# Merge, second norm and output rows of a two-layer graph attention kernel turned on VectorE and by DMA instead of on TensorE

## The chip, the cores and the metric

The kernel runs on 1 core of one Trainium2 chip. The metric is the device time of one launch in microseconds (us), read as the median of the runs. A core has TensorE (PE, with its weight loads PEld), VectorE (DVE), ScalarE (ACT), GpSimd (POOL), and SyncE (SP), which here only issues DMAs. All values are fp32.

## The reference, cut to what matters

16 graphs of 1024 nodes with 256 features share one adjacency matrix. Each goes through two residual blocks:

```python
h = maximum(layernorm(x), 0)                  # first norm
r = relu(h @ mlp1_w + mlp1_b)                 # 256 -> 512
a = elu(attention(r, no mask, W_fc))          # dense attention, 512 wide
r = elu(a) + r                                # the merge
r = relu(r @ mlp2_w + mlp2_b)                 # 512 -> 256, the output rows
a = elu(attention(r, adj, W_hand))            # masked attention A
x = x + relu(elu(a) + r)
h = maximum(layernorm(x), 0)                  # second norm
x = x + relu(attention(h, adj, L1_W))         # masked attention B
```

An attention is softmax over sources j of leaky_relu(f1[i] + f2[j]), times the projected rows.

## The kernel before

A graph's rows lie in SBUF either as nodes on the 128 partitions (natural) or as features on the partitions (turned). Matmuls that project features need the turned form, so the kernel turns data several times per graph. With 1024 nodes there are NT = 8 tiles of P = 128 nodes, in NH = 2 halves of TH = 4 tiles; 256 features are FC = 2 chunks, 512 are HC = 4.

**Stages of one graph.** `BlockNorm` or `Norm` makes the first norm; `Dense.mlp1` (line 743) makes `resT`, turned. `Dense.project` (754) makes natural rows `h_nat`. The dense attention has no mask, so it is not done as products of 1024 x 1024 weights (but for half of graph 0): the sources are ranked by their score (`rank`, 802), scattered in sorted order to HBM (`scatter`), read back, turned into running sums (`sum_before`, `sum_behind`), and written as tables; each node then fetches two rows by indirect DMAs on GpSimd (`gather`, 925; lines 934 in the profile). `mean` (951) combines them to natural rows `hp` of 513 values. `merge` (1001) turns four tiles of `hp` by four PE transposes into a PSUM bank per feature chunk, takes min with 0 on DVE (1008), two exponentials on ACT (1009, 1010), which give elu(elu(.)) up to a constant; `merge_end` (1013) joins them on DVE (1016) and adds them to `resT` on POOL (1017). `mlp2` (1019) makes `oT`, turned. `Masked.project` (605) uses `oT` as the stationary operand. `natural` (1030) turns `oT` back by four PE transposes per pair of tiles and ACT copies it out as `o_nat` (1040). The masked attention A makes weights on DVE (`weight`, 663, eight buffers deep) and products on PE (`product`, 672); `combine` and `add` (705, 706) add `o_nat` on POOL, `update` adds to x. The second norm is a `Norm`: statistics, `center` (526) on DVE, `turn` (529) with PE transposes (536) into PSUM, relu copy on ACT (540). Masked attention B follows the same way with `wl_sb`.

**First norm of graphs 3 to 15.** This one is a `BlockNorm` already: ACT centers and applies relu (565), DVE's transpose turns each 32 x 32 block in place (572), and 16 DMAs per half, issued by SP (582), carry each block to its place, in runs of 128 bytes.

**What sets the order.** The work of all graphs is a list of steps with due times in us, written with `at(name, lo, hi, steps)`; a table `SHIFT` corrects single due times. PERIOD (142) is the nominal distance of two graphs. The list is sorted by due time and traced in that order. PE, DVE, ACT and SP each keep exactly that order (`manual_schedule`, line 1397), and POOL is held to it as well (scatters among themselves excepted). So a due time decides only what stands ahead of what in an engine's queue. An instruction that is not ready holds back all that is behind it on its engine. The stages of several graphs are interleaved: while one graph is in its masked attentions, the next is in its table stage, and the one after that in its first projection.

**Buffers that matter.** `tr` PSUM has 2 banks, `mm` PSUM 4. `hT` has one buffer, shared in time by `oT` and the turned second norm. `onat` has one, `hp` four tiles, `hn` four tiles.

Of the kernel before, what the change touches and what calls it, by code (L numbers as in the profile page):

```python
# [28 lines left out]
D_MIN = 1.0e-7  # L29
SHIFT = {  # L30
    "end dense_begin1": (-2.54,),
    "end dense_begin2": (-0.99,),
    "end dense_begin4": (9.79, 10.84, 0, 0, 0, -3.05, 0, -5.96,),
    "end dense_begin5": (-23.89, -15.67,),
    "end dense_begin6": (-20.81, 0, -12.64, -10.02, -11.47, -12.26,),
    "end dense_begin7": (-3.07,),
    "end dense_end1": (-7.17, -1.95,),
    "end dense_end2": (-6.38, -6.38, -6.38, -6.38,),
    "end dense_rows1": (-10.51, -6.24, -6.82, 0, 0, 0, 0, -4.24,),
    "end dense_sums1": (-48.96,),  # L40
    "end dense_sums10": (-21.95,),
    "end dense_sums2": (8.53, 0, 0, 3.76, -8.53, -12.13, -7.88, -5.24,),
    "end dense_sums3": (-9.59, -12.4,),
    "end dense_sums4": (-7.91, -7.91, -7.91, -7.91, -3.45, -3.45, -3.45, -3.45,),
    "end dense_sums6": (10.61,),
    "end dense_sums7": (-3.22, -4.43, -3.58, -3.26, 0, -0.77, 0, 4.02,),
    "end dense_sums8": (3.76,),
    "end dense_sums9": (2.37,),
    "end early_gathers2": (10.03, 10.03,),
    "end early_gathers3": (-5.29, 18.84, 14.56, 18.48,),  # L50
    "end early_gathers4": (0, 0.45, 0, 0, 10.2, 15.36, 8.86, 10.63,),
    "end first_mlp1": (-7.09, 0, 0, -10.32,),
    "end first_mlp2": (-4.41, -4.41, -4.41, -4.41,),
    "end masked_first1": (-9.1,),
    "end masked_first10": (0, 0.7, -4.33, -3.67, -2.03, -1.81, -3.41,),
    "end masked_first11": (0, 0, -4.93, -4.17, -2.96, -1.43, -4.36, -0.47,),
    "end masked_first12": (0, -1.5,),
    "end masked_first13": (0, 0, -4.74, -4.15, 0, 0.69, 1.51, 0.6,),
    "end masked_first14": (0.61, 3.4, -2.77, -2.71, 0.32, 3.65, 1.3, 0.83,),
    "end masked_first15": (-2.98,),  # L60
    "end masked_first16": (0.15,),
    "end masked_first2": (-8.7,),
    "end masked_first4": (-7.99,),
    "end masked_first5": (-9.93, -3.59, -1.25,),
    "end masked_first7": (-18.06, 0, 3.52, 24.98,),
    "end masked_first9": (-2.7, -2.7, -2.7, -2.7, -2.7, -2.7, -2.7, -2.7, -1.13, -0.9, -1.12,
        -1.51, -1.92, -2.78, -3.21, -3.56, -4.22, -2.23, -1.85, -1.53, -1.76, -2.17, -2.28, -2.05,
        -5.73, -5.67, -4.93, -4.1, -4.46, -4.69, -5.08, -4.71, -7.38, -5.64, -6.02, -5.94, -4.67,
        -3.38, -2.99,),
    "end masked_second1": (0, 0, 0, 0, 0, 0, -2.7, -2.7, -2.7, -2.7, -2.7, -2.7, -4.75, -4.45, 0,  # L70
        0, 0, 0, 0, 1.61, 1.54, 3.47, 3.07, 3.3, -3.32, -2.79, 0, 0, 0, 0.67, -6.09, -6.45, -6.84,
        -3.49, 0, 2.45,),
    "end masked_second2": (0, 0, 0, 0, 0, 0, 3.2, 2.96, 0.23, 0.23, 0, 2.22,),
    "end masked_second3": (-0.67, -0.43, 0, 0, -0.54, 3.58, 2.58, 1.28,),
    "end masked_second4": (0, 0, 0, 0, 0, 2.18, 2.56, 4.8,),
    "end masked_second5": (14.49, 8.09, 12.75, 21.36, 24.19, 12.45,),
    "end masked_second6": (0, 17.47,),
    "end merges1": (-2.65, -5.36, -2.83, -5.06, 0, 2.68, 2.67, 0.66,),
    "end merges2": (-2.65, -5.24, 5.1, 1.49, 3.05, 1.93, 4.16, 11.78,),
    "end scatters1": (8.25, 10.06, -7.13, -3.44, -5.23, -10.63, 0, -8.12,),  # L80
    "end second_mlp1": (1.82, 4.66, 8.88, 11.17,),
    "end second_mlp2": (-9.26, -9.26, -9.26, -9.26, -9.26, -9.26, -9.26, -9.26,),
    "end second_mlp3": (-9.24,),
    "end second_norm1": (-4.45, -1.81, -4.63, -4.57, -4.39, -5.31, -5.93, -6.31,),
    "end second_norm2": (-6.82,),
    "end second_norm3": (-6.84,),
    "end second_norm4": (-7.95,),
    "end second_norm5": (-8.56, -3.63, -2.16, -3.25, -3.33, -6.23, -7.8,),
    "end second_norm6": (-7.46,),
    "end second_norm8": (0, 0, 0, 0, 31.85,),  # L90
    "end turn_at1": (-3.4, 0, 0, -4.89, -0.78, -0.78, -0.78, -0.78,),
    "end turn_at2": (0, 0, 0, 0.78, -1.37, -1.37, -1.37, -1.37,),
    "end weights a": (-5.34, -5.34, -5.34, -5.34, -5.34, -5.34, -5.34, -5.34, -1.3, -1.76, -8.73,
        -6.94, -1.68, -8.23, 0, 1, 0.15, 0, 0, 0, -7.3, 1.55, 0, 0, -2.46, -12.74, -3.66, -1.38,
        -1.88, -1.72, -2.61, -5.89, -4.74, -29.97, -2.33, -12.21, -4.28, -4.33, -3.77, -7.66,),
    "end weights b": (-7.6, -7.02, -8.62, -8.6, -3.43, -3.15, -2.16, 1.28, -7.9, -5.17, -3.12,
        1.84, 1.74, 2.72, -12.96, -7.11, -4.91, -8.89, -1.88, -2.69, -5.62, -3.89, -12.92, 1.63,
        -4.21, 0, -3.79, 0, 0, 2.74, 0.99, 2.24, -1.57, 0, -4.21, -0.92, -1.67, 0, 3.31, 2.71,
        -4.74, -4.74, -4.74, -4.74, -4.74, -4.74, -4.74, -4.74,),
    "first dense_begin1": (-4.48,),  # L100
    "first dense_begin2": (-2.87,),
    "first dense_begin3": (-3.83,),
    "first dense_begin4": (0, 0, 0, 0, 3.89, 0, 0, -2.44,),
    "first dense_begin5": (-21.03,),
    "first dense_begin6": (0, -31.1, -17.42, 4.95, -36.3, -14.56,),
    "first dense_begin7": (82.37,),
    "first dense_begin8": (7.54,),
    "first dense_end2": (0, 0, 2.75, 0, 0, 0, 0.57,),
    "first dense_rows1": (-3.65, 7.43, 4.91, 2.63, 0, -6.58, -11.11, -13.44,),
    "first first_mlp1": (-2.95, 0, 23.52,),  # L110
    "first first_mlp2": (1.92, 1.92, 1.92, 1.92,),
    "first first_norm3": (-20.91, -5.96, -6.07, -3.96, -21.09, -13.48, -23.18, -24.87,),
    "first first_norm4": (-5.5,),
    "first first_norm5": (0, -5.77, -1.25, -11.69,),
    "first first_norm6": (0, 0, 0, 0, 11.68, 18.8, 11.89,),
    "first first_norm7": (24.88, 40.1, 28.15, 35.87,),
    "first first_norm8": (26.12, 24.89, 20.85, 23.62,),
    "first gathers1": (0, 0, 0, 0, -16.12, 15.29, 10.43, 15.06,),
    "first gathers2": (5.92, 5.92, 5.92, 5.92, -11,),
    "first masked_first1": (-5.71,),  # L120
    "first masked_first10": (0, 0, 0, -2.4, -2.31, -5.55, -2.46, -3.12,),
    "first masked_first11": (0, 0, 0.71, -2.32, -2.78, -4.87, -2.51, -3.56,),
    "first masked_first13": (1.26, -0.54, -1.35, -6.25, -3.52, -7.85, -6.5, -7.52,),
    "first masked_first14": (3.16, 4.53, -1.81, -2.01, -1.61, -2.14, -7.33, -7.83,),
    "first masked_first15": (-5.06,),
    "first masked_first16": (-8.17,),
    "first masked_first4": (-5.61,),
    "first masked_first9": (0, 0, 0, 0, 0, 0, 0, 0, -1.71, -1.71, -1.71, -1.71, -1.71, -1.71,
        -1.71, -1.71, -2.98, -2.63, -1.7, -2.54, -2.61, -2.64, -3.51, -4.14, -3.57, -3.57, -3.57,
        -3.57, -3.57, -3.57, -3.57, -3.57,),  # L130
    "first masked_second1": (-14.06, -8.94, -9.49, -4.7, -3.33, -3.94, -2.72, -2.72, -2.72, -2.72,
        -2.72, -2.72, 0, 0, 0, 0, 0, 0, -2.18, -2.01, -2.79, -3.55, -3.29, -2.87,),
    "first masked_second2": (-3.14, -3.14,),
    "first masked_second3": (-3.5, -2.57, 0, 0.84, 7.19, 0.39, 33.41, 2.67,),
    "first masked_second4": (0, 0, 20.11, 7.6, 22.77, 6.57, 53.75, 28.92,),
    "first masked_second6": (32.22, 65.4,),
    "first merges1": (6.27, -3.15, 0, 3.13, 0, -2.78,),
    "first merges2": (3.91, -4.92, 0, 1.15, 3.24, -0.48, -0.83, 2.62,),
    "first scatters1": (0, 0, 0, 0, 0, 4.56, 0, -6.46,),
    "first second_mlp1": (-1.44, 0, 17.3, 6.53,),  # L140
    "first second_mlp2": (-5.85, -5.85, -5.85, -5.85, -5.85, -5.85, -5.85, -5.85,),
    "first second_norm1": (0, 2.5, 3.9, 8.4, 1.01, 0, 0.77,),
    "first second_norm2": (4.83,),
    "first second_norm6": (2.78,),
    "first second_norm7": (-8.87,),
    "first second_norm9": (-2.96,),
    "first start51": (-9.84,),
    "first turn_at1": (-11.5, -11.5, -11.5, -11.5, -7.26, -7.26, -7.26, -7.26,),
# [130 lines left out]
def fast_path(ctx: ExitStack, tc: tile.TileContext, alarm, x, adj, w1, b1, w2, b2, w_fc, a_fc,  # L279
# [942 lines left out]
    def last(b, n=1):  # L1222
        return b >= NB - n
# [633 lines left out]
```

## Time and profile before

| what | value |
|---|---|
| median of 2 runs | 2250.68 us (2250.66 to 2250.7) |
| the profiled execution, its own time | 2251.37 us |
| its span, first to last instruction | 2249.6 us |
| mean granted TensorE clock | 0.998 |
| distance of two graphs (issues of `rowsb` by SP at 514.41 and, ten graphs on, at 1858.81) | 134.4 us |
| HBM read and written | 226.88 MB and 126.29 MB |

How to read it: a line of the groups names line, engine and operation, out<-in, shape and count, then the group's busy time in us and the mean of one instruction in ns, then the idle time ahead of it and what ended it. The mean of a matmul is its latency; matmuls overlap, so the slot that one takes is read from the distance of two starts in the timeline. A line of the windows gives the busy us of each engine in that stretch. The chain of waits is followed back from the last instruction to whatever released each step.

### The profile page before, as it was taken

To read this page: it belongs to the slowest core of one execution; us is meant where nothing else is said; L and a number is where in the kernel's file an instruction comes from. 1 tells how busy PE (TensorE), PEld (TensorE's weight loads), DVE (VectorE), ACT (ScalarE), POOL (GpSimd) and SP (SyncE) were. 2 spreads that over 40 slices of the span, in tenths; PEclk is the share of its full clock that TensorE was granted. 3 is DMA by queue.
4 is the path that set the end of the run, shared out by engine and by line. 5 is a ranking of instruction groups with operands and counts; after the bars stand their busy time and mean duration, and the time that the engine had idled before them with its cause. 6 is when DMAs were issued, how large, how long until landed. Compare 5 with 4: busy or idle time off the path is not lost.

```text
span 2249.6 us, 31025 instructions
## 1 busy us (share of the span) xinstructions
PE 2207.2 (98%) x9754; PEld 1723.4 (77%) x9754; DVE 1643.1 (73%) x4535; ACT 1259.6 (56%) x2797; POOL 954.4 (42%) x1212
## 2 busy tenths in 40 slices
PE   7999999999999999999999999999999999999997
PEld 5767777787877878787787877878787787877776
DVE  7677676777867678776776867677786776858765
ACT  5355745547365564756557375564746557365542
POOL 1163425263452536425263452636435263543620
PEclk9999999999999999999999999999999999999999
DMA  5568466675766757566685666757566585645700
GB/s 197 159 175 196 114 208 154 186 183 148 197 123 200 187 168 190 137 196 148 192 191 147 189 127 194 188 177 189 130 205 144 185 197 153 164 125 169 178 22 28
DMA packets 263870, 368.95 MB, mean 164 GB/s; under 512 B 124352, under 2 KB 175880, under 8 KB 259600
## 3 DMA queue, kind: packets, MB, share of 16 engines
q1 hardware_dynamic: 217088, 202.72, 31.9%
q0 software_dynamic: 45952, 163.99, 28.9%
q8 instruction: 80, 1.31, 0.3%
q14 instruction: 94, 0.77, 0.1%
q10 hardware_dynamic: 656, 0.17, 0.0%
HBM read 226.88 MB, written 126.29 MB: 157 GB/s over the span
## 4 chain that ended last, share of the span: by engine, by line
PE 75%; DVE 6%; DMA 2%; POOL 2%; ACT 1%; issue 1%; POOLq 0%; DVEq 0%; ACTq 0%; SPq 0%
PE oa L677 17%; PE h L762 16%; PE ob L677 14%; PE m L1024 8%; PE m L748 6%; PE pa L614 4%; PE pb L614 3%; PE hpT L1006 2%; DMA got<-coarse,k 2%; DVE attb L667 1%; PE carry L918 1%; PE on L1038 1%; PE nt L536 1%; DVE stats L516 1%; DVE hp L959 1%
## 5 line engine op out<-in xcount | busy, mean ns | idle before, releaser
L677 PE MATMUL ob<-hmb,attb 128*128 128x257 f32 x2048 | 463.9, 380 | 2.2 <-DVE attb L667 1.9
L762 PE MATMUL h<-wfc_sb,resT 128*128 128x257 f32 x2048 | 462.8, 379 | 0.0
L677 PE MATMUL oa<-hma,atta 128*128 128x258 f32 x2048 | 459.9, 382 | 1.8 <-DVE atta L667 1.5
L677 PEld LDWEIGHTS ob<-hmb,attb 128*128 128x128 f32 x2048 | 383.9, 190 | 67.2 <-issue 12.3
L677 PEld LDWEIGHTS oa<-hma,atta 128*128 128x128 f32 x2048 | 384.8, 190 | 59.3 <-DVE atta L667 2.9
L762 PEld LDWEIGHTS h<-wfc_sb,resT 128*128 128x128 f32 x2048 | 380.1, 189 | 59.1 <-issue 7.4
L705 POOL TENSOR_TENSOR posa<-posa,onat 128x256 f32<-128x256 f32 x118 | 106.7, 904 | 546.1 <-ACT posa L693 487.6
L667 DVE SCALAR_TENSOR_TENSOR attb<-rowsb,qwdb,edge 128x256 f32<-128x256 f32 (+1 forms) x536 | 292.1, 563 | 34.6 <-PE ob L677 28.6
L667 DVE SCALAR_TENSOR_TENSOR atta<-rowsa,qwda,edge 128x256 f32<-128x256 f32 (+1 forms) x520 | 257.3, 524 | 51.4 <-DMA rowsa<-row_a 35.6
L934 POOL DMA_INDIRECT got<-coarse,k x124 | 203.4, 1640 | 90.9 <-DMA got<-fine,k 56.6
L748 PE MATMUL m<-hT,w_sb 128*128 128x512 f32 x512 | 236.6, 596 | 1.9 <-ACT rb L719 1.1
L1024 PE MATMUL m<-resT,w_sb 128*128 128x512 f32 x512 | 228.3, 593 | 1.0 <-POOL resT L1017 1.0
L719 ACT ACTIVATE rb<-ob,recb 128x256 f32<-128x256 f32 x128 | 58.5, 474 | 274.9 <-DVE recb L717 248.9
L1017 POOL TENSOR_TENSOR resT<-resT,e 128x512 f32<-128x512 f32 x128 | 165.5, 1295 | 104.9 <-DVE e L1016 96.7
L692 ACT ACTIVATE ea<-oa,reca 128x256 f32<-128x256 f32 x128 | 60.3, 471 | 248.1 <-DVE reca L689 228.7
L934 POOL DMA_INDIRECT got<-fine,k x124 | 126.7, 1022 | 128.5 <-DVE hpd L999 41.9
L1024 PEld LDWEIGHTS m<-resT,w_sb 128*128 128x128 f32 x512 | 94.5, 190 | 102.4 <-issue 93.5
L748 PEld LDWEIGHTS m<-hT,w_sb 128*128 128x128 f32 x512 | 94.2, 191 | 89.0 <-issue 74.7
L822 POOL DMA_INDIRECT sorted<-hnat,place x128 | 128.6, 1004 | 53.9 <-DVE place L815 33.0
L764 ACT COPY hnat<-h 128x257 f32<-128x257 f32 x256 | 90.8, 367 | 104.1 <-PE h L762 101.6
L845 ACT ACTIVATE junk<-r,fs 128x1024 int8<-128x1024 f32 x124 | 142.6, 1150 | 0.9 <-POOL fs L766 0.6
L1016 DVE SCALAR_TENSOR_TENSOR e<-hpT,e 128x512 f32<-128x512 f32 x128 | 87.9, 688 | 53.2 <-ACT e L1010 53.0
(195 smaller groups left out, 3391.2 us busy)
## 6 DMA issues: line engine op xcount, KB each, us to landing
xs<-sorted SPq DMA_DIRECT2D x32, 1028.0 KB
fine<-tt SPq DMA_DIRECT2D x32, 1026.0 KB
fine<-xs SPq DMA_DIRECT2D x32, 1026.0 KB
x<-in_x_dram SPq DMA_DIRECT2D x16, 1024.0 KB
xn<-in_x_dram SPq DMA_DIRECT2D x15, 1024.0 KB
out_dram<-x SPq DMA_DIRECT2D x28, 512.0 KB
hT<-xn SPq DMA_DIRECT2D x416, 32.0 KB
coarse<-carry SPq DMA_DIRECT2D x32, 256.5 KB
```

Of the source, the lines that this page charges most:

```text
L614: nc.tensor.matmul(ps[:, :2 + F], lhsT=hT[:, c, t * P:(t + 1) * P], rhs=self.w_sb[:, c, 0, :], start=(c == 0), stop=(c == FC - 1))
L667: nc.vector.scalar_tensor_tensor(a_t[:, :n * P], self.rows[:, i], self.qwd[:, 1, j:j + 1], edge[:, j, i], op0=OP.max, op1=OP.mult)
L677: nc.tensor.matmul(self.out[t][:, :F + self.ONES], lhsT=self.att[t0, j][:, (t - t0) * P:(t - t0 + 1) * P], rhs=self.hm[:, j, 2:2 + F + sel ...
L705: adder.tensor_add(pos, pos, o_nat[:, t, :])
L748: nc.tensor.matmul(ps, lhsT=w1_sb[:, kc, c * P:(c + 1) * P], rhs=piece(kc, h), start=(kc == 0), stop=(kc == FC - 1))
L762: nc.tensor.matmul(ps[:, :F + 1], lhsT=self.resT[:, kc, t * P:(t + 1) * P], rhs=wfc_sb[:, kc, g, :], start=(kc == 0), stop=(kc == HC - 1))
L764: nc.scalar.copy(self.h_nat[:, t, g, :], ps[:, :F + 1])
L822: made = nc.gpsimd.indirect_dma_start(out=sorted_d[self.b % 2], out_offset=bass.IndirectOffsetOnAxis(ap=self.place[:, t:t + 1], axis=0), i ...
L845: nc.scalar.activation(junk, self.r2, AF.Sign, bias=self.fs[:, 0, t:t + 1], accum_out=self.signs[:, t:t + 1])
L934: nc.gpsimd.indirect_dma_start(out=got[u // n][:, u % n, :], out_offset=None, in_=(coarse_d if coarse else fine_d)[self.b % 2][:, :], in_o ...
L1017: nc.gpsimd.tensor_add(dst, dst, e)
L1024: nc.tensor.matmul(ps, lhsT=w2_sb[:, kc, c * P:(c + 1) * P], rhs=self.resT[:, kc, h * HALF:(h + 1) * HALF], start=(kc == 0), stop=(kc == H ...
```

## The change

For graphs 1 to 13 three turns leave PE. The merge: `mean` writes in place in the gathered rows, `elu` works on natural rows, `turn` joins and block-transposes them on DVE, `move_means` carries blocks by 16 DMAs per half (each 32 partitions x 2 KB, one run each) to `landed`, and `add_means` adds them to `resT` on POOL. The output rows: `oT` is block-transposed in place, and 32 DMAs of 1 KB runs carry it to `o_nat`. The second norm becomes a `BlockNorm`. The moves of the first norm now carry 1 KB runs too, from a buffer `hx` of their own. To have long runs, the turned tensors are laid out by (node block, chunk, tile, node in block); a tile of sources then holds the nodes of one 32-block of each of four tiles, so the masks' source axis and the rows `qwd` are permuted to match. Graphs 0, 14 and 15 keep the PE turns; there `natural` copies its permuted operand straight on DVE first. The constant -1 of the elu moves from the output rows to the two updates. Nearly all entries of `SHIFT` are new; the diff below is cut, of that table only the entries of the middle graphs that the text speaks of are kept.

```diff
+HX = 1
 SHIFT = {
...
-    "mid dense_begin5": (-5.41,),
-    "mid dense_begin6": (-11.19, 0, -28.74, -20.88, -19.69, -15.58,),
-    "mid dense_rows1": (0, -1.19, 11.53, 8.91, -6.51, -4.58, 0, -7.8,),
-    "mid second_mlp1": (2.88, 3.81, 13.47, 11.19,),
...
+    "mid dense_begin5": (7.35, -28.14,),
+    "mid dense_begin6": (-15.45, -9.73, -31.73, -9.78, -5.27, -19.16,),
+    "mid dense_rows1": (-4.31, -5.97, 11.22, 4.24, -10.86, -1.79, 0, -5.11,),
+    "mid means2": (-4.12, -2.71, -0.7, -1.84,),
+    "mid means3": (0, 0, 0, 0, 6.87, 6.87, 6.87, 6.87,),
+    "mid means4": (0, 0, 0, 0, 7.4, 2.85, 9.59, 6.9,),
+    "mid second_mlp1": (0, 0, 4.72, 2.31,),
...
     def build_masks(t):
...
-        nc.vector.tensor_scalar(valid, valid, wrong[:, 1, t:t + 1], None, op0=OP.max)
+        by_tile = work.tile([P, N], BF16, tag="e2", name=f"by_tile_{t}", bufs=3)
+        for h in range(NH):
+            lo = h * HALF
+            nc.vector.tensor_scalar(
+                by_tile[:, lo:lo + HALF].rearrange("p (a u i) -> p u a i", u=TH, i=Q),
+                valid[:, lo:lo + HALF].rearrange("p (u a i) -> p u a i", u=TH, i=Q),
+                wrong[:, 1, t:t + 1], None, op0=OP.max)
...
+        def rows(self, t):
+            h, u = divmod(t, TH)
+            if u == 0:
+                self.hn[h] = big.tile([P, TH * F], F32, tag="hx", name=f"hx{self.name}_{h}", bufs=HX)
+            return self.hn[h]
...
         def center(self, t):
...
+            hx = self.rows(t).rearrange("p (q c u i) -> p u c q i", q=P // Q, c=FC, i=Q)
+            nc.scalar.activation(hx[:, u], self.get_x()[:, t].rearrange("p (c q i) -> p c q i",
+                                                                        c=FC, i=Q),
+                                 AF.Relu, bias=self.shift[:, t:t + 1], scale=self.rstd[:, t:t + 1])
+
+        def blocks(self, h):
+            nc.vector.transpose(self.hn[h], self.hn[h])
...
-            for q in range(P // Q):
-                nc.sync.dma_start(dst[q * Q:(q + 1) * Q, :, a, :],
-                                  src[a * Q:(a + 1) * Q, :, q, :])
...
+            move_blocks(self.hT[:, h], self.hn[h], a)
+
+    def move_blocks(dst, src, a, width=FC * HALF):
+        run = width // (P // Q)
+        for q in range(P // Q):
+            nc.sync.dma_start(dst[q * Q:(q + 1) * Q, a * run:(a + 1) * run],
+                              src[a * Q:(a + 1) * Q, q * run:(q + 1) * run])
+
+    def sources(wide, c, t):
+        h, a = divmod(t, TH)
+        lo = (a * FC + c) * P
+        return wide[:, h, lo:lo + P]
+
+    def by_rows(t):
+        return t.rearrange("p (a c u i) -> p c u a i", a=P // Q, c=FC, i=Q)
...
+            part, hp = got[:, :K], got[:, K:]
+            nc.scalar.activation(part, part, AF.Copy, scale=den[:, 1, u:u + 1])
...
+        def elu(self, h, u):
+            e = self.parts[h, u] = work.tile([P, 2, F + 1], F32, tag="e2",
+                                             name=f"e_{self.b}_{h}_{u}", bufs=3)
+            e = e.rearrange("p s f -> p (s f)")[:, :K]
+            nc.scalar.activation(e, self.hps[h, u], AF.Relu, scale=-1.0)
+            nc.scalar.activation(e, e, AF.Exp, scale=-1.0)
+            nc.scalar.activation(e, e, AF.Exp, bias=neg1)
+
+        def turn(self, h, u):
+            if u == 0:
+                self.turned = big.tile([P, TH * K], F32, tag="hp", name=f"hx_{self.b}_{h}",
+                                       bufs=1)
+            wide = self.parts.pop((h, u))
+            e = wide.rearrange("p s f -> p (s f)")[:, :K]
+            nc.vector.scalar_tensor_tensor(e, self.hps[h, u], 0.0, e, op0=OP.max, op1=OP.add)
+            dst = self.turned[:, :TH * H].rearrange("p (q s c u i) -> p u s c q i", q=P // Q, s=2,
+                                                    c=FC, i=Q)[:, u]
+            for i in range(2):
+                nc.vector.transpose(dst[:, i],
+                                    wide[:, i, :F].rearrange("p (c q i) -> p c q i", c=FC, i=Q))
+
+        def move_means(self, h, a):
+            if a == 0:
+                self.landed = big.tile([P, NH * FC * HALF], F32, tag="onat",
+                                       name=f"land_{self.b}_{h}", bufs=1)
+            move_blocks(self.landed, self.turned, a, TH * H)
+
+        def add_means(self, h, c):
+            dst = self.resT[:, c, h * HALF:(h + 1) * HALF].rearrange("p (u a i) -> p u a i", u=TH,
+                                                                    i=Q)
+            src = self.landed.rearrange("p (a c u i) -> p c u a i", a=P // Q, c=HC, i=Q)[:, c]
+            nc.gpsimd.tensor_add(dst, dst, src)
...
+        def blocks(self, h):
+            nc.vector.transpose(self.oT[:, h], self.oT[:, h])
+
+        def move(self, h, a):
...
+            move_blocks(self.o_nat[:, h], self.oT[:, h], a)
...
+                    nodes = by_rows(self.oT[:, h])[:, c, u0 + u]
+                    line = work.tile([P, P], F32, tag="e1", name=f"line_{self.b}_{q}_{u}_{c}")
+                    nc.vector.tensor_copy(line.rearrange("p (a i) -> p a i", i=Q), nodes)
+                    nc.tensor.transpose(ps[:, u * F + c * P:u * F + (c + 1) * P], line, ident)
...
-        norm2[b] = Norm(lambda b=b: xs[b], b, 1)
+        norm2[b] = (BlockNorm if 0 < b < NB - 2 else Norm)(lambda b=b: xs[b], b, 1)
...
-            merges(t0 + late + 85 + 13.2 * h, d, h)
+            lo = t0 + late + 85 + 13.2 * h
+            if last(b, 2):
+                merges(lo, d, h)
+                continue
+            at("means1", lo - 5, lo - 2, each(d.elu, [h], range(TH)))
+            at("means2", lo - 3, lo, each(d.turn, [h], range(TH)))
+            at("means3", lo + 0.5, lo + 2, each(d.move_means, [h], range(P // Q)))
+            at("means4", lo + 6, lo + 8, each(d.add_means, [h], range(HC)))
...
+                at("masked_first8", t0 + 0.5, t0 + 2, each(d.blocks, range(NH)))
+                at("masked_first8b", t0 + 3, t0 + 13, each(d.move, range(NH), range(P // Q)))
...
-            n.turn_at(t0 + 60.3, 0, 7)
-            n.turn_at(t0 + 67.3, 1)
-            lo = t0 + 71
+            for h, start in enumerate((47.0, 60.0)):
+                start += t0
+                at("second_norm_shift", start, start, [partial(n.shifts, h)])
+                at("second_norm_center", start + 0.5, start + 2, [partial(n.center, t) for t in tiles(h)])
+                at("second_norm_blocks", start + 3, start + 3, [partial(n.blocks, h)])
+                at("second_norm_move", start + 3.2, start + 5, each(n.move, [h], range(P // Q)))
+            lo = t0 + 77
```

## The prediction, as it went on record

> **What bounds the kernel now.** The page comes first: busy time, the slices, the chain.
>
> ```profile
> PE 2207.2 (98%) x9754; PEld 1723.4 (77%) x9754; DVE 1643.1 (73%) x4535; ACT 1259.6 (56%) x2797; POOL 954.4 (42%) x1212
> ...
> PE   7999999999999999999999999999999999999997
> ...
> PE oa L677 17%; PE h L762 16%; PE ob L677 14%; PE m L1024 8%; PE m L748 6%; PE pa L614 4%; PE pb L614 3%; PE hpT L1006 2%; DMA got<-coarse,k 2%; DVE attb L667 1%; PE carry L918 1%; PE on L1038 1%; PE nt L536 1%; DVE stats L516 1%; DVE hp L959 1%
> ```
>
> PE is full in all slices but the ends, and the chain runs along PE, its transposes (hpT, on, nt) included. Matmul ends are modelled, so next the timeline of PE, for real slots:
>
> ```profile
> 1110.69 0.60 PE L1038 MATMUL on<-ident,oT 128*128 128x128 f32 x4
> 1111.13 7.13 PE L677 MATMUL oa<-hma,atta 128*128 128x258 f32 x32
> ...
> 1194.78 3.60 PE L1024 MATMUL m<-resT,w_sb 128*128 128x512 f32 x8
> ...
> 1200.17 1.03 PE L1006 MATMUL hpT<-ident,hp 128*128 128x128 f32 x8
> 1201.04 3.60 PE L1024 MATMUL m<-resT,w_sb 128*128 128x512 f32 x8
> ```
>
> Four transposes hold PE 0.44 us, eight 0.87: 0.109 us each, not the 272 ns latency of the group line. Between clusters there is no gap. A 257-column product takes 0.2175 us, one of 512 columns 0.43. Third, windows over one graph, for what comes next once PE has less to do (columns: PE, PEld, DVE, ACT, POOL, clock, DMA share, GB/s):
>
> ```profile
> 1110.00:1120.00 10.00, 10.00 (x51) 8.75 (x51) 10.00 (x25) 3.26 (x8) 0.95 (x1) 1.00 0.47 140
> 1120.00:1130.00 10.00, 10.00 (x49) 8.58 (x49) 8.54 (x17) 5.70 (x14) 5.06 (x7) 1.00 0.40 107
> 1130.00:1140.00 10.00, 10.00 (x48) 8.74 (x47) 9.83 (x31) 4.00 (x11) 5.34 (x7) 1.00 1.02 220
> 1140.00:1150.00 10.00, 10.00 (x48) 8.77 (x47) 8.46 (x21) 4.33 (x12) 8.41 (x11) 1.00 0.79 256
> 1150.00:1160.00 10.00, 10.00 (x48) 7.99 (x47) 9.66 (x36) 2.76 (x6) 7.83 (x7) 1.00 0.81 213
> ```
>
> PE is unbroken, but in the masked attentions DVE is busy 46.5 of 50 us: the runner-up. Last, the groups that price the change:
>
> ```profile
> L1017 POOL TENSOR_TENSOR resT<-resT,e 128x512 f32<-128x512 f32 x128 | 165.5, 1295 | 104.9 <-DVE e L1016 96.7 <-DVE recb L717 8.0
> L1008 DVE TENSOR_SCALAR e<-hpT 128x512 f32<-128x512 f32 x128 | 84.9, 682 | 54.8 <-PE hpT L1006 49.6 <-POOL resT L1017 2.9 <-PE line_ps L496 1.2
> L526 DVE TENSOR_SCALAR hn<-x,mv,rstd 128x256 f32<-128x256 f32 x128 | 49.6, 422 | 7.0 <-POOL rstd L522 6.9
> L572 DVE STREAM_TRANSPOSE xn<-hn 128x256 f32<-128x256 f32 x104 | 42.4, 427 | 0.0
> ```
>
> **What the Trainium skill says.** "TensorE: Matmul & The Clock Gate", Part 4: a PE transpose turns a full 128x128 into PSUM, about 275 ns in a kernel; the trace agrees as latency (272), while its slot is 109. "VectorE: DVE Perf Modes", The three transpose paths: DVE turns 32x32 blocks only; so DMAs have to follow. "SBUF — State Buffer", Door 1, the note on cachelines: an access with at least two hits per 16-byte line is at full rate; the new operands run 128 bytes, so I take matmuls that read them strided as no slower. No row here shows such a read.
>
> **What is removed from PE.** Per graph 2 x 4 x 4 transposes of the merge, 16 of the output rows, 16 of the second norm: 64. 13 x 64 x 0.109 = 90.7 us. No product is added.
>
> **DVE, per graph.** Gone: 8 min at 0.682 (L1008), 8 joins at 0.688 (L1016), 8 centers at 0.422: 14.3 us. New: 8 joins of 513 at 0.75 (as L959), 16 transposes at 0.427, two in-place transposes of 1024 each for output rows and second norm. From 427 ns at 256 and about 1.05 ns per element (682 ns at 512 against 422 at 256) one of 1024 takes about 1.22: four, 4.9. The first norm's eight at 0.427 become two at 1.22: -1.0. Shifts 0.4. Sum +17.1, net +2.8. The row L572 already writes strided blocks; if the finer patterns cost double, +13 more. Taken: no more.
>
> **ACT, per graph.** Gone: exponentials 8 x (0.626 + 0.722), output copies 4 x 0.679, norm copies 4 x 0.594: 15.9. New: 8 x (0.72 + 0.626 + 0.722) and 8 centers at 0.595 (L565): 21.3. Net +5.4 on 77 of 134: under PE.
>
> **POOL.** `add_means` is 8 adds of the old size, in 32-value pieces: between 1.295 and double, 0 to 10.4 us per graph, on 61 of 134. Taken: 1.295. POOL also issues the gathers: those of the second half stand behind the adds of the first (5.2 us), and `mean` on DVE waits for them.
>
> **SP and DMA.** Issues per graph go from 32 to 128 moves. The old ones take 609 ns; SP's one-run issues (rowsb) 320. So 19.5 becomes 41 us of SP's 127. The trace's packet records give 12.2 ns per 128-byte packet, 54.9 for 1 KB, 120 for 2 KB: 106496 x 12.2 goes, 39936 x 54.9 and 13312 x 120 come: over 16 engines -81 + 237 = +156 us, from 61% to some 70%. Behind moves that wait for DVE stand on SP the row broadcasts, table writes and stores; SP already stands 44 us per graph at rowsb (575 us over 13, SP's waits), so it has room. The masked products wait for the rows, the gathers for the tables.
>
> **Where the moved latency goes.** After the last join a half now needs two transposes (0.86), 16 issues (5.3), landing, four adds (5.2). No row gives an SBUF landing: a row written to HBM took 1.25 us from ACT's issue (1185.43) to SP's dependent one (1186.68); "DMA: Bandwidth & Descriptors", Anatomy of one DMA, states about 2.0. Taken 1.6; sum 13.0 us, then `mlp2` starts. PE's cover, by the due times of middle graphs in the diff: first half, last turn 82.8 to `mlp2` 102.5: seven `project` steps of 8 x 0.2175 and two of second-norm projection (0.87), 13.9 us. Second half, 97.45 to 117.7: six `project` and two `mlp2` steps (3.44), 17.3. Just enough: I charge 0.5 us per graph. With no cover a half costs about 12.5.
>
> In the masked attentions DVE gets +2.4 (output rows) +2.4 -3.4 (second norm) on 46.5: 48.0, while PE, less its 20 transposes there, needs 47.8. DVE has held 98 to 100% in two of those slices with PE full. At 98%: 49.0, 1.2 us late per graph; at its average of 93%: 51.6, 3.8 late. The att buffers run dry and the products are late next. Taken: 1.2.
>
> Ends: the masks' eight steps become two strided halves each (0 to 7 us in the start; 2 taken); the DVE copies ahead of PE transposes in graphs 0, 14, 15 (48 of about 0.29, mostly hidden; 2 taken, 14 at most).
>
> **Sum.** Span 2249.6 - 90.7 + 13 x 1.7 + 4 = 2185; the profiled execution lies 1.8 above its span and the median 0.7 below that: 2186 us.
>
> **Rivals.**
> A, the forecast: PE stays the bound, 2152 to 2205. 2160 is the sum with no new wait; the 42 us in which PE idles now (2249.6 - 2207.2), most of them in the first and the last slice, may move by some 8 either way under the new order of the ends, hence 2152.
> B, DVE becomes the bound in the masked attentions: 3.8 instead of 1.2, 2186 + 34 = 2220; up to 2245 if patterns or adds cost more. For: the 100% slices. Against: DVE idles a quarter of a graph, elsewhere.
> C, slower: the handover of the means is exposed, `mlp2` standing in PE's queue behind DMAs. One half each graph uncovered: 2250.7 - 90.7 + 13 x 12.5 = 2322. It turns to a loss from 7.0 us per graph (90.7/13), to over 2% from 10.4. For: the cover of the first half barely equals the need, and late tables on SP would add. Against: PE has no wait of this kind now.
> D, the strided moving operand slows `mlp1` (512 x 0.43 = 220 us): 10% is 22 us, 2208; 41% would eat all. That the transposes cost nothing is excluded by the gapless timeline.
>
> **Chances.** A 0.60, B 0.17, D 0.06, C 0.17 (of it 0.12 past +2%). About 2% is what a measurement of this kernel tells from no change: 2206 and 2296. Faster: A, 0.04 of B, 0.02 of D: 0.66. Slower 0.12. Same 0.22. Range for 8 in 10: 2152 to 2245, which leaves out C and a little below; A's own is 2152 to 2205.
>
> **What would show it.** Right: 832 fewer PE transposes, PE at 96% or more, two graphs 127 to 129 us apart, idle of PE ended by DVE att in single us per graph. Wrong: PE idle ended by POOL `resT` or by `landed` (C); masked products waiting for att throughout (B); m<-hT over 0.43 us in its slot (D); group means of `turn` or `add_means` near double.

## The result, and the profile after

The changed kernel takes 2633.48 us (two runs, 2628.91 and 2638.06) against 2250.68: a ratio of 1.170, 95% interval 1.161 to 1.179. The forecast was 2186, faster; the sign is wrong. The profiled execution took 2628.91 us, with a span of 2627.2. From its page, the busy time of the engines, the slices of PE and of its clock, and the lines of the chain that ended last:

```profile
PE 2266.6 (86%) x8922; PEld 1676.4 (64%) x8922; DVE 1670.4 (64%) x4591; ACT 1327.3 (51%) x2913; POOL 953.4 (36%) x1212
...
PE   8998888978799787997879978789787997989998
...
PEclk9999999989999898998999989899898998989999
...
SPq L624 15%; PE oa L726 12%; DMA hT<-hx 7%; PE h L813 6%; PE ob L726 3%; DMA xs<-sorted 3%; DVE atta L716 3%; DVE attb L716 2%; PE m L1113 2%; DVE junk L861 2%; PE pb L661 2%; DMA rowsa<-row_a 2%; DMA r<-row_r 2%; DVE junk L859 2%; DMA sorted<-hnat,place 2%
```

PE runs 832 instructions fewer, as intended, but is 86% busy instead of 98%, and 24 of its 40 slices are below 90%. The chain, three quarters of which lay on PE before, now has SP's issue of the block moves (`move_blocks`, L624) as its largest single entry. So the question is what PE waits for. From PE's waits (what PE waited for, us in all, times, the longest):

```profile
PE pb L661 <- ACT resT L802: 74.4, 11, 8.4
PE pb L661 <- DMA hT<-hx: 64.3, 22, 5.0
PE m L1113 <- POOL resT L1048: 42.6, 20, 4.2
```

L661 is the projection of the second norm's rows for masked attention B: 163.9 us of PE's waits stand ahead of it (1.5 before the change), more than ahead of any other group. The waits of `mlp2` (L1113) for the added means come second. The chain shows one wait of L661 (start, us, what), from SP's last move of the first half to PE:

```profile
1353.01 8.11 DMA hT<-hx
1361.30 2.07 ACT hx L608 x4
1363.37 0.58 ACT resT L802
1363.99 3.77 PE pb L661 x8
```

ACT can center the second norm's second half only when the single buffer `hx` is free, that is when the first half's moves have landed. These landed 8.1 us after the last was issued, while the DMA engines were 97% busy (1350 to 1364). Behind the centers ACT's list has the copies of `mlp1` (`resT`, L802), whose PSUM banks PE needs; so the wait carries their name.

The mean granted clock is 0.947 instead of 0.998. It falls after idle stretches, as windows of one stretch show (columns as in the prediction; the share ahead of "DMA share" is the clock):

```profile
1206.00:1216.00 10.00, 5.43 (x15) 4.09 (x14) 7.71 (x18) 7.60 (x14) 0.00 (x0) 0.56 0.54 115
1216.00:1226.00 10.00, 10.00 (x44) 8.57 (x44) 0.83 (x4) 4.77 (x11) 0.28 (x2) 0.93 0.42 104
```

In the first, PE idles nearly half of the time and the clock is 0.56. The 32 products that begin at 1213.18 take 9.18 us, 0.287 each on average where the kernel before needs 0.2175. The clock's records show full or half speed only; half speed covers 277 us of the span, and PE is busy in 188 of them.

That gives the balance. PE's work should be 2207.2 - 90.7 = 2116.5 us; its busy time is 2266.6, so 150 more. The half clock in 188 busy us accounts for 94 of these. The other 56 are not the clock: PE's work now falls into 267 unbroken stretches instead of 47, each of which ends with a product's whole latency (some 0.38 us) instead of its slot (0.2175), which by this estimate is 36 us; the rest is open. Idle time of PE went from 42.4 to 360.6, so the waits cost 318. Together -90.7 + 150 + 318 = 377.6, the difference of the spans.

The timeline of SP shows one stretch (start, us, line, DMA, count):

```profile
1215.05 10.01 SPq L624 DMA_DIRECT2D land<-hx  x16
1231.66 10.95 SPq L624 DMA_DIRECT2D hT<-hx  x16
1242.71 10.23 SPq L624 DMA_DIRECT2D land<-hx  x16
1252.99 0.58 SPq L832 DMA_DIRECT2D r<-row_r  x1
1253.67 0.40 SPq L777 DMA_DIRECT2D out_dram<-x  x1
1254.12 0.50 SPq L699 DMA_DIRECT2D rowsb<-row_b  x1
```

Sixteen moves hold SP 10 to 11 us, 0.63 to 0.68 each. From 1231.66 SP does nothing but moves for 21 us; only then come the row of scores that VectorE's ranking of the next graph waits for (`r`), a store, and the row of masked attention B (`rowsb`). POOL's timeline shows the other end of the two moves of the means:

```profile
1226.70 6.62 POOL L1048 TENSOR_TENSOR resT<-resT,land 128x512 f32<-128x512 f32 x4 [7.00 <-DMA land<-hx]
...
1254.73 1.26 POOL L1048 TENSOR_TENSOR resT<-resT,land 128x512 f32<-128x512 f32 x1 [6.55 <-DMA land<-hx]
```

The first half's last turn on DVE starts at 1214.21, its adds end at 1233.32: 19.1 us. The second half's starts at 1237.31; SP is still at the first norm's moves (`hT`) until 1242.61, so the moves begin 4.6 us late, and the adds end at 1260.39: 23.1 us.

### The profile page after: what moved, and what is told of

Its sections match the earlier page's. It is cut to its first block, busy times and chain, and to the rows that moved or that the text cites. A ratio compares the mean times of both kernels' runs of the same rounds, so it can differ in the third digit from the quotient of the medians.

```text
span 2627.2 us, 31317 instructions
## 1 busy us (share of the span) xinstructions
PE 2266.6 (86%) x8922; PEld 1676.4 (64%) x8922; DVE 1670.4 (64%) x4591; ACT 1327.3 (51%) x2913; POOL 953.4 (36%) x1212
## 4 chain that ended last, share of the span: by engine, by line
PE 31%; DVE 20%; DMA 18%; SPq 15%; ACT 6%; issue 5%; POOL 5%; DVEq 0%; ACTq 0%; POOLq 0%
SPq L624 15%; PE oa L726 12%; DMA hT<-hx 7%; PE h L813 6%; PE ob L726 3%; DMA xs<-sorted 3%; DVE atta L716 3%; DVE attb L716 2%; PE m L1113 2%; DVE junk L861 2%; PE pb L661 2%; DMA rowsa<-row_a 2%; DMA r<-row_r 2%; DVE junk L859 2%; DMA sorted<-hnat,place 2%
## 5 line engine op out<-in xcount | busy, mean ns | idle before, releaser
L726 PE MATMUL ob<-hmb,attb 128*128 128x257 f32 x2048 | 482.8, 385 | 22.7 <-ACT rb L769 9.9
L813 PE MATMUL h<-wfc_sb,resT 128*128 128x257 f32 x2048 | 485.6, 392 | 7.8 <-ACT hnat L815 7.2
L813 PEld LDWEIGHTS h<-wfc_sb,resT 128*128 128x128 f32 x2048 | 399.9, 197 | 85.3 <-issue 13.3
L661 PE MATMUL pb<-wl_sb,hT 128*128 128x258 f32 x512 | 164.7, 477 | 163.9 <-ACT resT L802 74.4
L1113 PE MATMUL m<-resT,w_sb 128*128 128x512 f32 x512 | 249.8, 633 | 43.0 <-POOL resT L1048 42.6
L716 DVE SCALAR_TENSOR_TENSOR attb<-rowsb,qwdb,edge 128x256 f32<-128x256 f32 (+1 forms) x536 | 255.9, 499 | 26.1 <-DMA rowsb<-row_b 14.4
L661 PEld LDWEIGHTS pb<-wl_sb,hT 128*128 128x128 f32 x512 | 118.4, 241 | 208.3 <-ACT resT L802 83.8
L1048 POOL TENSOR_TENSOR resT<-resT,land 128x512 f32<-128x512 f32 x104 | 145.0, 1415 | 205.5 <-DMA land<-hx 197.9
L1113 PEld LDWEIGHTS m<-resT,w_sb 128*128 128x128 f32 x512 | 99.9, 202 | 162.2 <-issue 92.7
L1014 DVE SCALAR_TENSOR_TENSOR got<-got,den 128x513 f32<-128x513 f32 x108 | 86.1, 820 | 165.4 <-ACT got L1006 165.4
L613 DVE STREAM_TRANSPOSE hx<-hx 128x1024 f32<-128x1024 f32 x52 | 64.5, 1240 | 184.9 <-ACT hx L608 164.5
L817 POOL COPY fs<-hnat 128x1 f32<-128x1 f32 x128 | 29.1, 227 | 395.3 <-ACT hnat L815 390.0
```

The costliest lines, as they stand in the source:

```text
L613: nc.vector.transpose(self.hn[h], self.hn[h])
L661: nc.tensor.matmul(ps[:, :2 + F], lhsT=part(c, t), rhs=self.w_sb[:, c, 0, :], start=(c == 0), stop=(c == FC - 1))
L716: nc.vector.scalar_tensor_tensor(a_t[:, :n * P], self.rows[:, i], self.qwd[:, 1, j:j + 1], edge[:, j, i], op0=OP.max, op1=OP.mult)
L726: nc.tensor.matmul(self.out[t][:, :F + self.ONES], lhsT=self.att[t0, j][:, (t - t0) * P:(t - t0 + 1) * P], rhs=self.hm[:, j, 2:2 + F + sel ...
L813: nc.tensor.matmul(ps[:, :F + 1], lhsT=self.resT[:, kc, t * P:(t + 1) * P], rhs=wfc_sb[:, kc, g, :], start=(kc == 0), stop=(kc == HC - 1))
L1014: nc.vector.scalar_tensor_tensor(out, hp, den[:, 0, u:u + 1], part, op0=OP.mult, op1=OP.add)
```

## The experiments

**The theories.** T1: what costs is the number of issues on SP. The queue is in order, 128 moves of 0.63 us hold it 81 us per graph, and the row broadcasts, table writes and reads behind them are late. T2: what costs is the latency of each handover (moves, landing, GpSimd's adds) and the single buffer `hx`, whoever issues. T3: the new table of corrections is a bad order for this kernel, and the order is to blame.

**1. One DMA per half.** The changed kernel with the 16 moves of each half of the three new turns replaced by one DMA of the same bytes; it leaves out the exchange of 32-row blocks between partitions. The first norm keeps its 32.

```diff
-            move_blocks(self.hT[:, h], self.hn[h], a)
-
-    def move_blocks(dst, src, a, width=FC * HALF):
+            move_blocks(self.hT[:, h], self.hn[h], a, one=self.tag == "hT")
+
+    def move_blocks(dst, src, a, width=FC * HALF, one=True):
         run = width // (P // Q)
+        if one:
+            if a == 0:
+                nc.sync.dma_start(dst[:, :width], src[:, :width])
+            return
```

> The changed kernel, but each half of the merge, of the second norm and of the output rows goes out as one DMA of the whole tile in place of 16 (same bytes; what is left out is the exchange of the 32-row blocks, so the rows land in wrong places). The first norm keeps its 32 moves. Theory 1 (issue on SP: a move holds SP for 0.63 us, 128 of them per graph stand in one queue ahead of the row broadcasts and table writes): 90 issues fewer per graph, the 26 us per graph that the chain spends in SP's moves go, 2627 - 13 x 26 = 2290 or less, towards 2190 where PE is the bound again and its clock recovers. Theory 2 (latency: landings, the adds on POOL and the single buffer hx that ACT waits for hold up PE, however many issues there are): a landing stays, so at most a third of the loss comes back, 2500 or more.

Measured: 2503.5 us, 125 to 130 less. T1's number failed clearly, T2's held. In its trace the means' DMA is issued at 1307.79 and the adds start at 1314.17: 6.4 us where the 16 issues and their landing take 11.65. The second half still stood behind the first norm's 16 moves. Most of what came back did not come from the means, though: PE's waits ahead of the second norm's projection fall from 163.9 to 48.2 us, those ahead of `mlp2` from 43.0 to 0.5, while others grow (ahead of the projection for masked attention A, `pa`, from 13.2 to 34.5). With this table, then, few issues shorten the handovers, that of the second norm above all, and 250 us of the loss stay.

**2. Issues alone, in the kernel before.** Each of its 32 moves of the first norm is cut in four: 128 issues per graph, the same bytes, runs, results and engine work.

```diff
-                nc.sync.dma_start(dst[q * Q:(q + 1) * Q, :, a, :],
-                                  src[a * Q:(a + 1) * Q, :, q, :])
+                for v in range(0, 8, 2):
+                    nc.sync.dma_start(dst[q * Q:(q + 1) * Q, v:v + 2, a, :],
+                                      src[a * Q:(a + 1) * Q, v:v + 2, q, :])
```

> The kernel before, with each of its 32 moves of the first norm cut into four (128 issues per graph, same bytes, all else the same, PE's transposes included). Theory 1: two stretches of SP grow from 10 to 40 us, the broadcast of the rank rows and those of masked attention A stand behind them: 30 to 60 us more per graph, 2250 + 13 x 45 = 2830 (2640 to 3030). Theory 2: nothing else changes, 2250 to 2290.

Measured: 2866.2 us, 613 more, 47 per graph, with a clock of 0.904; that is in T1's range. Two blocks in SP's timeline:

```profile
1342.03 41.26 SPq L583 DMA_DIRECT2D hT<-xn  x64
1383.33 0.58 SPq L782 DMA_DIRECT2D r<-row_r  x1
1384.02 42.28 SPq L583 DMA_DIRECT2D hT<-xn  x64
```

The ranking's row waits behind 41 us of moves. SP still waits 573.0 us in all for `rowsb`, as in the kernel before (575.0): its free time is untouched, and the loss is there anyway. So T1's mechanism alone can cost more than the whole loss.

**3. The price of an issue.** A kernel that leaves out the whole computation and issues 16 DMAs of one kind after another.

> Only DMAs, in groups of 16 issues (it computes nothing of the reference): SBUF to SBUF of 32 partitions x 1 KB, of 128 partitions x 1 KB, of 32 partitions x 8 runs of 128 bytes, of 32 partitions x 2 KB, HBM to SBUF of 32 and of 128 partitions, and two of them from ACT. Theory 1: an issue costs 0.5 to 0.6 us whenever it covers 32 partitions, whatever its bytes, and about 0.32 with 128 partitions. Theory 2: the 0.59 us of the changed kernel is a queue that is full of bytes; alone all are near 0.32.

From its timeline, first from SBUF to SBUF on 32 partitions x 1 KB, then the same from HBM to SBUF:

```profile
17.96 11.01 SPq L35 DMA_DIRECT2D small<-src  x16
...
90.26 7.29 SPq L51 DMA_DIRECT2D load<-there  x16
```

Sixteen take 11.01 and 7.29 us. Also from SBUF to SBUF: 10.20 on 128 partitions, 10.94 with the 1 KB in eight runs, 11.14 with 2 KB. So one takes 0.64 to 0.70 us there, whatever the partitions, runs and bytes, and 0.46 where one side is HBM (7.31 for 16 in the other direction). ACT's queue takes 0.64 to 0.78. A price by partitions (T1's detail) and one by a full queue (T2's) both fail. In the first group the landing takes 1.35 us from the end of the last issue.

**4 to 7. The tables emptied.** Both kernels with `SHIFT` empty, the changed one also with all three turns back on PE, and with one DMA per half as in experiment 1 (which leaves out the exchange again).

```diff
 SHIFT = {
-    "end dense_begin2": (-0.15,),
...
 }
```

> The kernel before with an empty table of corrections: each step stands at its nominal due time. Theory 1 (SP's issues in one queue make the loss) and theory 2 (latency and the single buffer) say nothing of it but that it is the base for the runs beside it: 2280 to 2400. Theory 3 (the changed kernel is slow since its table of corrections orders the queues badly) needs the corrections to be worth much: 2400 or more.

> The changed kernel with an empty table of corrections. Theories 1 and 2: the loss is in what is issued and waited for, not in the corrections, so it lies 250 to 450 us above the plain kernel before (some 2700). Theory 3: it is as fast as the changed kernel or faster (2630 or less), and within 100 us of the plain kernel before.

> The changed kernel with an empty table, with merge, second norm and output rows of all graphs back on PE; the new layout, the permuted sources, the buffer hx, the 32 first-norm moves of 1 KB and a DVE copy ahead of each PE turn of the output rows stay. Theories 1 and 2: the loss goes with the three turns, within 60 us of the plain kernel before. If the layout itself costs (strided operands, hx), it stays over 100 us above.

> As the changed kernel with an empty table, with one DMA of the whole tile per half in place of 16 for the three new turns (the exchange of the 32-row blocks is left out). Theory 1: 90 issues fewer per graph give back 100 to 350 us against the one with 16, as the same edit gave 125 under the full table. Theory 2: 60 us or less.

Measured: before 2364.3, changed 3096.7, turns back on PE 2450.4, one DMA per half 2601.9. T3 falls: the changed kernel's table saves it 463 us, the kernel before's 114, so without tables the gap is not smaller but 732 us. Its parts, each a difference of two runs: 495 for issuing 96 moves per graph instead of six (3096.7 - 2601.9), 151 for what the six leave of the moved turns, the PE saving taken in (2601.9 - 2450.4), 86 for layout and the DVE copies ahead of PE's transposes (2450.4 - 2364.3; with the turns on PE, PE waits 65.9 us for those copies). The three terms add up because they telescope; each rests on single runs. The forecasts of T1 and T2 missed here: run 5 lies 732 above run 4 instead of 250 to 450, run 6 lies 86 above it instead of at most 60 (or over 100 if the layout costs), and what run 7 gives back, 495, exceeds T1's 350 and T2's 60. Each of the three turns has 32 issues, so the next three runs tell whether issues are all.

**8 to 10. One part alone.** From the kernel of run 6, only one of the three turns is moved.

```diff
-MEANS, OUT_ROWS, NORM2 = False, False, False
+MEANS, OUT_ROWS, NORM2 = True, False, False
```

> The changed kernel with the table of corrections empty, and of the three turns only the merge moved; output rows and second norm stay on PE. To be set against the same layout with all three on PE (2450) and with all three moved (3097). T1 (issues on SP): each part adds 32 issues of about 0.65 us, 20 us of SP per graph, so each alone costs something like a third of the 647 us or less (the first 32 find some free time on SP): 2500 to 2670, and the three parts alike. T2 (latency of the handover): the merge has 16 DMAs and four adds between rank and the second projection and bears most of the loss: 2700 or more, the other two near 2450. The copies between output queues or partitions play no part in either.

> As the run before, but only the second norm moved. T1: 2500 to 2670, like the merge alone, for it has as many issues, and its buffer hx is shared with the first norm. T2: near 2450, since nothing of the table stage waits for it by landing.

> As before, but only the output rows moved; these are needed late (POOL adds them to x), so no engine waits for their landing. T1: still a loss from 32 issues on SP, 2450 to 2600, because the row broadcasts and tables of the next graph stand behind them. T2: no loss, 2430 or less, since 16 transposes per graph leave PE (22.7 us in all) and nothing waits.

Measured: 2835.3, 2717.3 and 2538.1: 385, 267 and 88 us over 2450.4. Together 740 against 646 for all three at once, so they nearly add. T1's "alike" is wrong, and two of the three lie above its 2670; T2's 2700 for the merge held, its "near 2450" for the norm and the rows is wrong. Each part costs, and not by its number of issues, which is the same; PE's waits show that each holds up something else. In the run with the means PE waits longest ahead of `mlp2` (12 times, 212.5 us, put down to ACT's `lineb`, and 65.0 to `resT`); in the one with the norm, ahead of the projection for masked attention B (217 us, put down to ACT); with the rows, for masked weights from DVE (150).

**11. Output rows alone in the kernel before.** Its own layout and table, 16 moves of 32 partitions x 16 runs of 128 bytes per graph (`MOVE_AT` is 7).

```diff
+        def blocks(self, h):
+            part = self.oT[:, :, h * HALF:(h + 1) * HALF]
+            nc.vector.transpose(part, part)
...
+            for q in range(P // Q):
+                nc.sync.dma_start(dst[a * Q:(a + 1) * Q, :, q], src[q * Q:(q + 1) * Q, :, a])
...
+            at("rows_blocks", t0 + 0.5, t0 + 0.5, each(d.blocks, range(NH)))
+            at("rows_move", t0 + MOVE_AT, t0 + MOVE_AT, each(d.move, range(P // Q)))
```

> The kernel before with its own layout and table, with only the output rows of graphs 1 to 13 turned by two in-place block transposes on DVE and 16 DMAs of 32 partitions x 16 runs of 128 bytes per graph (instead of 32 DMAs of 1 KB). It computes the reference. PE loses 13 x 16 x 0.109 = 22.7 us. T1: 16 issues are 10.5 us of SP per graph, less than its free time per graph, put where SP waits for DVE: the gain of PE remains in part, 2228 to 2255; if even these hold up the row broadcasts, 2270. T2: nothing waits for the landing, 2228.

Measured: 2342.0, ratio 1.041 (1.039 to 1.042). With the 22.7 us that PE saves, 113 us went, 8.7 per graph. Both theories had forecast at most 2270, so both missed. SP's timeline and its largest wait:

```profile
1281.99 0.32 SPq L657 DMA_DIRECT2D rowsa<-row_a  x1
1282.40 10.98 SPq L1051 DMA_DIRECT2D onat<-oT  x16
...
1294.15 1.07 SPq L908 DMA_DIRECT2D fine<-tt  x2
```

```profile
SPq L657 <- DMA row_b<-lineb: 650.1, 13, 56.7
```

The table writes (`fine`) went out 1.3 us after `rowsa` in the kernel before (1233.92, 1235.19) and go out 12.2 us after it here. SP has 50 us per graph at `rowsb` to spare, more than before, but at another place of its list.

**12. The same moves, issued by GpSimd.**

```diff
-                nc.sync.dma_start(dst[a * Q:(a + 1) * Q, :, q], src[q * Q:(q + 1) * Q, :, a])
+                nc.gpsimd.dma_start(dst[a * Q:(a + 1) * Q, :, q], src[q * Q:(q + 1) * Q, :, a])
```

> The kernel before with the output rows of graphs 1 to 13 turned by block transposes and the same 16 moves per graph at the same due time as the run with them on SP (2342), but issued by GpSimd, which in the kernel before stands idle for 29 us there (waiting for ACT posa) while SP is at the tables. T1 (what costs is the place in SP's in-order queue): the 90 us loss goes, 2230 to 2260, since SP's list is that of before again. T2 (what costs is the latency of the moved rows, or DVE's 2.4 us per graph in the masked attention): the loss stays, 2320 or more. If GpSimd needs well over 1.8 us for an issue of 512 runs, it overflows its 29 us and a part of the loss comes back: 2260 to 2340.

Measured: 2280.7, ratio 1.014 (1.012 to 1.016), between T1's range and T2's. 61 us came back, so the place in SP's queue cost at least about that much of the 113 (more, if the issues on GpSimd have a cost of their own). The rest is in POOL's timeline:

```profile
1249.46 8.47 POOL L1051 DMA_DIRECT2D onat<-oT  x13 [7.84 <-issue]
1258.17 0.65 POOL L1051 DMA_DIRECT2D onat<-oT  x1 [0.24 <-DMA onat<-oT]
1261.87 0.65 POOL L1051 DMA_DIRECT2D onat<-oT  x1 [3.04 <-DMA onat<-oT]
...
1272.52 0.72 POOL L711 TENSOR_TENSOR posa<-posa,onat 128x256 f32<-128x256 f32 x1 [8.86 <-DMA onat<-oT]
```

An issue takes GpSimd 0.65 us, no more than SP, but after thirteen it waits for earlier moves, and the add that needs the rows waits 8.9 us after the last issue. So this is not the slow issue that the third forecast (2260 to 2340) had in mind. In these microseconds the tables, 1 MB per DMA, are written.

**13. The means' moves of the changed kernel issued by GpSimd**, and **14. the first norm's `hx` freed early** (its block transpose writes back into the norm's own x).

```diff
-            move_blocks(self.landed, self.turned, a, TH * H)
+            move_blocks(self.landed, self.turned, a, TH * H, nc.gpsimd)
```

```diff
-            nc.vector.transpose(self.hn[h], self.hn[h])
+            dst = self.hn[h]
+            if self.own:
+                dst = self.get_x()[:, half(h)].rearrange("p t f -> p (t f)")
+            nc.vector.transpose(dst, self.hn[h])
+            self.hn[h] = dst
```

> The changed kernel with the 32 moves of the means per graph issued by GpSimd, which adds them afterwards, instead of SP. The same DMAs, one fewer part on SP. T1: SP is freed of 32 x 0.63 = 20 us per graph, so up to 262 us less than 2633: 2370 to 2500 if GpSimd issues one in about 1 us, since they stand just ahead of its own adds. T2 (handover latency): GpSimd issues no faster than SP, so the handover is as long or longer: 2600 or more.

> The changed kernel with the first norm's block transpose writing from hx back into the norm's own x buffer, so that the single buffer hx is free after the transpose instead of after 16 moves have landed. T1: ACT's wait for hx (150 us in all) is a follow-on of SP's late moves, so little comes back: 2570 to 2640. T2 (single buffer hx binds): up to 150 us, 2480 to 2550.

Measured: 2715.4 and 2629.7. The first is 82 us slower with 32 issues fewer on SP: T2's number, not T1's. Its second half's moves start 7.9 us after the last turn on DVE (1262.93 to 1270.81), and the adds end at 1290.93, 28.8 us after that turn began; PE's wait for `resT` went from 42.6 us to 138.6. The order was not adapted to the new queue, so this tells only that freeing SP does not help while the handover grows. The second shows that the first norm's use of the single `hx` costs nothing that these runs tell apart. The second norm's use stays: ACT still waits 92.0 us for `hx` there, and PE 157.6 ahead of the second norm's projection. A buffer of its own for the second norm was not tried.

**15. Run 12 with DVE's two transposes later**, in a 4.2 us wait of DVE behind the scores.

```diff
-            at("rows_blocks", t0 + 0.5, t0 + 0.5, each(d.blocks, range(NH)))
+            at("rows_blocks", t0 + 5.6, t0 + 5.6, each(d.blocks, range(NH)))
```

> As the kernel before with the output rows moved by GpSimd (2281), but the two block transposes (2.4 us on VectorE) stand after the scores and three table steps of VectorE, where it waits 4.2 us for the row broadcast in the kernel before, instead of ahead of the scores that this broadcast waits for. If what remained of the loss (2281 against 2228) is VectorE's place in the chain scores -> row -> weights, it falls by up to 2.4 x 13 = 31 us: 2245 to 2260, perhaps with the whole PE saving 2228. If it is the latency of 16 moves from GpSimd ahead of the adds, it stays at 2270 to 2290.

Measured: 2358.8, ratio 1.046 (1.044 to 1.049), outside both forecasts. In one graph the moves now start 7.5 us after the last step of the scores on DVE, where in run 12 they started with it, and GpSimd has stood idle 14.7 us by then; the adds wait 8.7 us for the landing, DVE's updates wait for the adds (119.8 us in all), and PE then waits 9.5 us for masked weights (97.2 over the whole kernel, 21.8 in run 12). That suggests that in run 12 the landing of the rows was the binding step already, not DVE's place ahead of the scores. No version here beats the kernel before.

## Why the prediction was wrong, point by point

**The failed step: "So 19.5 becomes 41 us of SP's 127", and "so it has room".** Two errors stand in it. The size: a move was priced by `rowsb`, 0.320 us, as a one-run issue. But `rowsb` is a read from HBM that stands alone, and the old moves' 609 ns was the nearer row, being SBUF to SBUF in a row of issues. The moves take 0.63: 81 us per graph, not 41, though the runs are longer. The kind: SP's wait of 44 us at `rowsb` was taken as room. An in-order queue has room only at the place where it waits. Experiment 2 leaves that wait at 573 us and loses 613; experiment 11 lengthens it to 650 and loses 113 on 16 issues, of which 61 came back when GpSimd issued them.

**A second step that failed: "Where the moved latency goes" knows only the merge.** The second norm has a handover too: first half's moves, landing, `hx` free, ACT's centers, second half's moves. The prediction put it at nothing, without a reason. PE's largest waits stand there, 163.9 of 360.6 us, and with one DMA per half (experiment 1) they are 48.2. The landing read there was 8.1 us, not 1.6.

**"Just enough: I charge 0.5 us per graph."** The handover of the means was put at 13.0 us: turns 0.86, issues 5.3, landing 1.6, adds 5.2. Measured in one graph: 0.77, 10.0, 1.6 and 6.6, so 19.1, and 23.1 in the second half, where it stands 4.6 us behind another norm's moves. The landing of 1.6 was right here; the 2.0 of the Trainium skill ("DMA: Bandwidth & Descriptors", Anatomy of one DMA) is stated for DMAs that GpSimd issues, and these are issued by SP, so the two are not the same measure. Against the covers of 13.9 and 17.3 some 11 us per graph would be bare; PE's waits that carry the name `resT` are 42.6 us, 3.3 per graph, so the new order covers more than the prediction counted. This is rival C's mechanism, with a chance of 0.17; its price of 2322 was too low because it let only the means be late. In the trace the same issues also delay the ranking's row, the row of masked attention B and the second norm's projection.

**The clock** was not in the sum: the records account for 94 us, a fifth of the miss of 447. It was not to be had from the profile before, where PE idled 42 us in all and the clock's mean was 0.998.

**What was right.** 832 fewer PE instructions. DVE +27 us (36 forecast), ACT +68 (70), POOL -1 (0 taken). `add_means` 1415 ns, above the 1295 taken and far below double. The transposes of 1024 columns 1240 ns (1.22; the slope taken, 1.05 ns per element, is 1.02 by its own two rows, which changes nothing), and those of 256 columns in the finer pattern 424 ns (427):

```profile
L1048 POOL TENSOR_TENSOR resT<-resT,land 128x512 f32<-128x512 f32 x104 | 145.0, 1415 | 205.5 <-DMA land<-hx 197.9
...
L613 DVE STREAM_TRANSPOSE hx<-hx 128x1024 f32<-128x1024 f32 x52 | 64.5, 1240 | 184.9 <-ACT hx L608 164.5
```

Rival D is out: eight strided products of `mlp1` take 3.67 us, with 0.59 for the last one's latency 0.44 each, and sixteen take 7.03 us, 0.43 each, which agrees with the note on cachelines in the Trainium skill ("SBUF — State Buffer", Door 1). Rival B is out too: PE's waits for masked weights are 27 us in all, 2.1 per graph where 1.2 was charged, and they are small beside the rest. The busy times of DVE, ACT and POOL were in order; the errors lay in the queue whose time the page does not count as busy, and in what PE waits for.

**What stays open.** With the full tables the gap is 383 us, and experiment 1 accounts for 125 of it. How the other 258 divide between handovers, layout and the order is open; the shares of the kernels with empty tables (495 for issues, 151, 86) are of other orders. Whether the second norm's waits go when it has a buffer `hx` of its own is not shown. Of the 113 us of experiment 11, 61 belong to SP's queue; that the other 52 are the landing is what runs 12 and 15 suggest, but no run has the rows landing early without another change.

## What to carry to other kernels

Count the issues of a DMA change as work of the queue that issues them, at the price of the same kind of DMA in a row, and lay them out in that queue's order: what matters is what stands behind each block of issues, not how long the queue waits elsewhere. Turning half of the means cost PE sixteen transposes, 1.7 us in its pipeline; by block moves it is a handover of 19 us, which has to be covered by work that is already in the order. Price such a handover for every part that is moved, and for the buffer that its halves share. When the bound engine begins to wait, add what its clock will lose.

## What the runs showed of the hardware that was not expected

- An issue from SBUF to SBUF costs SP 0.63 to 0.70 us in a row and one with an HBM side 0.46, whatever the bytes (32 to 128 KB), partitions and runs in experiment 3.
- GpSimd issues a plain DMA of 512 runs in 0.65 us and one of 32 runs in 0.50. In the blocks read it went through 16 in a row once (run 13), and waited for earlier ones after 13 (run 12), 10 (run 13) and 8 (run 15).
- Block moves landed 1.6 us after their last issue in one place of the changed kernel and 8.1 us after it in another, where the DMA engines were 97% busy.
- The granted clock was full or half in every record. Its mean was 0.947, 0.904 and 0.873 with PE busy 86%, 80% and 76% of the span (changed kernel, experiments 2 and 5), but 0.896 with 83% (run 8), so the busy share alone does not set it. Gaps of 3.1 and 4.6 us in PE's work stand around the window at 0.56.
